# The end of a graph-attention loop written out as one list of stages

## Chip, cores, metric

The kernel runs on one core of a Trainium2 chip. The metric is device time in microseconds of one execution; the median of three runs is 2806.0 us (2797.12 to 2806.96).

## What is computed

One graph layer over 12500 nodes of 128 features and 200000 edges that are sorted by their destination:

```
h = relu(layernorm(x))
Q = h @ W_Q.T;  K = h @ W_K.T
score[e] = (Q[dst[e]] . K[src[e]]) / sqrt(128) * exp(-edge_weight[e])
keep the 16 highest scores of each destination node
alpha = softmax of the kept scores over a node's edges
agg[n] = sum over its kept edges of alpha[e] * (h[src[e]] @ W_msg.T)
out = x + relu(h @ W_self.T + agg)
```

## The kernel before

A preparation computes h into a table in DRAM (`h_tab`) and lays the edge arrays out by columns. Then the edges are worked off in G = 112 groups. A group is 14 chunks of 128 edges, and since a node's edges may reach into the next group, 15 chunks are looked at (`chunks[g]`); the last group, called L = G - 1 = 111 here, has 9. In what follows L-1, L-2 and so on are the groups ahead of it.

A group goes through these stages, each a small function that emits the instructions of one or two engines (lines of the profile in brackets):

- `gather` [L399, POOL]: one indirect DMA for each chunk, 128 rows of `h_tab` by the chunk's source indices; `let_go` [L414, DVE] copies the indices that release them. Group g's are issued during the loop pass of group g-2.
- `load_nodes`, `load_dst` [SP's DMAs], `far_of`, `to_edges` [L466, L471, ACT] and `places` [L477, L479, DVE]: the one-hot matrices that take node values to edges and edges to slots.
- `q_to_edges(g, b)` [L490, PE]: the query rows for four chunks, three matmuls a chunk, into one of three PSUM banks q. `scores(g, b)` [L500, DVE]: one instruction a chunk, the product of gathered row, query row and decay, summed. The instruction waits for its chunk's gathered rows.
- `scores_in_slots` [L508, DVE], `slots_by_node` [L513, L515, PE], `slots_out` [L520, ACT], `node_by_slots` [L523, PE]: the scores of a node's edges side by side in one row, in PSUM tile e.
- `best` [L529 to L541, DVE]: the 16 highest, and a mask with the negated maximum (`km`). `sum_of_exps` [L546, ACT], `one_over_sum` [L551, L552, DVE].
- `kept_to_edges` [L558, PE]: mask and maximum back to the edges, in PSUM tile x, of which there is one. `on_edges` [L564 to L571, DVE] reads it, `exps` [L575, ACT], `weights` [L579, L580, DVE] writes the weights into `alz`, of which there are two.
- `sums(g, 0)`, `sums(g, 1)` [L590, PE]: the weighted sums of gathered rows, two matmul passes a chunk, the first half of the chunks and the second. `sums_out` [L595, ACT], `sums_turned` [L598, PE], `sums_turned_out` [L602, ACT], `products` [L605, L606, PE], `output` [L610, DVE].
- `store` [L616 and L619]: a direct DMA on SP's queue for all but the last four groups; for groups L-3 to L a scattered DMA on POOL's queue, whose rows the program can't tell apart from those of other stores, so that each waits for the store ahead of it to land.

The order of instructions on each engine is the order in which the stages are called (`tc.manual_schedule()`, L386). It is written out by hand in the loop at L630: pass i calls stages of groups i+3 (loads) down to i-5 (output), interleaved so that each engine has work of several groups. The function `at` leaves out a stage whose group doesn't exist. The loop runs from -3 to G+5; passes L to L+6 have no gather left to release and wind the open groups up, each pass calling the stages in the same order: for group L the pass i = L, for L-1 `slots_by_node` first in that pass, for L-2 `best` to `on_edges`, for L-3 `weights` and `sums`, for L-4 `sums_turned` and `products`, for L-5 `output` and `store`. Where pass L has two stages of one engine, one group's waits hold up the other's[...].

After the loop comes a branch at L685 that is not taken with these inputs.

Of the kernel before, what the change touches and what calls it, by code (L numbers as in the profile page):

```python
# [38 lines left out]
TAIL = 4  # L39
# [35 lines left out]
def gnn_layer(  # L75
# [32 lines left out]
    LAST = N - (NT - 1) * P  # L108
    CH = -(-M // P)
    G = -(-CH // GC)  # L110
    assert G > TAIL
    EG = GC * P

    CPR = 13
# [271 lines left out]
    with tc.tile_pool(name="win", bufs=2) as win, tc.manual_schedule():  # L386
# [96 lines left out]
        def q_to_edges(g, b):  # L483
            j0, j1 = 4 * b, min(4 * b + 4, chunks[g])
            if j0 >= j1:
                return
            T[g]["pq", b] = pq = bank("q", 3)
            for j in range(j0, j1):
                for k in range(3):
                    nc.tensor.matmul(pq[:, (j - j0) * P:(j - j0 + 1) * P],  # L490
                                     lhsT=T[g]["to_e"][:, j * P:(j + 1) * P], rhs=upper(T[g]["q"][:, k, :]),
                                     start=(k == 0), stop=(k == 2))
# [18 lines left out]
        def slots_by_node(g):  # L511
            n = chunks[g]
            nc.tensor.matmul(et[0:KM + 1, 0:WW], lhsT=zrow[:, 0:KM + 1], rhs=zrow, start=True, stop=False)  # L513
            for j in range(n):
                nc.tensor.matmul(et[0:KM + 1, STEP * j:STEP * j + WN], lhsT=sl1[g % 2][:, j, :],  # L515
                                 rhs=T[g]["ow"][:, j, :], start=False, stop=(j == n - 1))

        def slots_out(g):
            T[g]["eT"] = win.tile([KM + 1, P], F32, name="eT")
            nc.scalar.copy(T[g]["eT"], et[0:KM + 1, PRE:PRE + P])  # L520

        def node_by_slots(g):
            nc.tensor.transpose(et[:, 256:256 + KM + 1], T[g]["eT"], ident[0:KM + 1, 0:KM + 1])  # L523


        def best(g):
            pt = et[:, 256:256 + KM + 1]
            ell = win.tile([P, KM], F32, name="ell")
            nc.vector.tensor_scalar(ell, slots, pt[:, KM:KM + 1], NEG, op0=OP.is_ge, op1=OP.mult)  # L529
            nc.vector.tensor_add(ell, ell, pt[:, 0:KM])  # L530
            T[g]["v16"] = v16 = win.tile([P, TOPK], F32, name="v16")
            rest = win.tile([P, KM], F32, name="rest")
            nc.vector.max(v16[:, 0:8], ell)
            nc.vector.match_replace(rest, v16[:, 0:8], ell, NEG)
            nc.vector.max(v16[:, 8:16], rest)
            nc.vector.match_replace(rest, v16[:, 8:16], rest, NEG)
            T[g]["km"] = km = win.tile([P, KM + 3], F32, name="km")
            nc.vector.tensor_scalar(km[:, KM:KM + 1], v16[:, 0:1], FLOOR, -1.0, op0=OP.max, op1=OP.mult)  # L538
            nc.vector.tensor_tensor(km[:, 0:KM], rest, ell, op=OP.not_equal)
            for k in range(KM, KM + 2):  # L540
                nc.vector.tensor_sub(km[:, k + 1:k + 2], km[:, k:k + 1], upper(km[:, k:k + 1]))  # L541
# [7 lines left out]
        def one_over_sum(g):  # L549
            T[g]["rden"] = rden = win.tile([P, 1], F32, name="rden", bufs=4)  # L550
            nc.vector.tensor_scalar(rden, T[g]["den"], 0.25, None, op0=OP.max)  # L551
            nc.vector.reciprocal(rden, rden)  # L552
# [8 lines left out]
        def on_edges(g):  # L561
            n, px = chunks[g], T[g]["px"]
            T[g]["up"] = up = win.tile([P, NJ], F32, name="up", bufs=3)
            nc.vector.tensor_reduce(up[:, 0:n], px[:, 0:n, KM:KM + 3], axis=AX.X, op=OP.add)  # L564
            nc.vector.tensor_add(up[:, 0:n], up[:, 0:n], T[g]["s"][:, 0:n])

            nc.vector.tensor_scalar(up[:, 0:n], up[:, 0:n], 0.0, None, op0=OP.min)  # L567
            mine = win.tile([P, NJ, KM], F32, name="mine", bufs=1)
            nc.vector.tensor_tensor(mine[:, 0:n, :], px[:, 0:n, 0:KM], T[g]["po"][:, 0:n, :], op=OP.mult)
            T[g]["kept"] = kept = win.tile([P, NJ], F32, name="kept", bufs=3)  # L570
            nc.vector.tensor_reduce(kept[:, 0:n], mine[:, 0:n, :], axis=AX.X, op=OP.add)  # L571

        def exps(g):
            n = chunks[g]
            nc.scalar.activation(T[g]["up"][:, 0:n], T[g]["up"][:, 0:n], AF.Exp)  # L575

        def weights(g):
            n, kept = chunks[g], T[g]["kept"]
            nc.vector.tensor_tensor(kept[:, 0:n], T[g]["up"][:, 0:n], kept[:, 0:n], op=OP.mult)  # L579
            nc.vector.tensor_tensor(alz[g % 2].rearrange("e (j w) -> e j w", w=WW + STEP)[:, 0:n, 0:WN],  # L580
                                    T[g]["ow"][:, 0:n, :], bc(kept[:, 0:n], WN), op=OP.mult)


        def sums(g, part):
            n = chunks[g]
            if part == 0:
                T[g]["pa"] = bank("a", 1)
            half = n // 2
            for j in range(half) if part == 0 else range(half, n):
                nc.tensor.matmul(T[g]["pa"][:, 0:P], lhsT=alz[g % 2][:, WW * j + PRE:WW * j + PRE + P],  # L590
                                 rhs=rows_of(g, j), start=(j == 0), stop=(j == n - 1))

        def sums_out(g):
            T[g]["agn"] = win.tile([P, D], F32, name="agn")
            nc.scalar.activation(T[g]["agn"], T[g]["pa"][:, 0:P], AF.Copy, scale=T[g]["rden"])  # L595

        def sums_turned(g):
            nc.tensor.transpose(so[:, 2 * P:3 * P], T[g]["agn"], ident)  # L598

        def sums_turned_out(g):  # L600
            T[g]["aggT"] = win.tile([P, P], F32, name="aggT")
            nc.scalar.copy(T[g]["aggT"], so[:, 2 * P:3 * P])  # L602

        def products(g):
            nc.tensor.matmul(so[:, 3 * P:4 * P], lhsT=T[g]["hT"], rhs=wselfT, start=True, stop=False)  # L605
            nc.tensor.matmul(so[:, 3 * P:4 * P], lhsT=T[g]["aggT"], rhs=wmsgT, start=False, stop=True)  # L606

        def output(g):
            T[g]["o"] = win.tile([P, D], F32, name="o")
            nc.vector.scalar_tensor_tensor(T[g]["o"], so[:, 3 * P:4 * P], 0.0, T[g]["x_t"],  # L610
                                           op0=OP.max, op1=OP.add)

        def store(g):

            if g < G - TAIL:
                nc.sync.dma_start(out[ds(start_of(g, 0, N - P), P), :], T[g]["o"])  # L616
            else:
                k = g - (G - TAIL)
                nc.gpsimd.indirect_dma_start(  # L619
                    out=out[:, :], out_offset=bass.IndirectOffsetOnAxis(ap=idxo[:, k:k + 1], axis=0),  # L620
                    in_=T[g]["o"], in_offset=None, bounds_check=N - 1, oob_is_err=False)

        def at(g, stage, *args):
            if 0 <= g < G:
                stage(g, *args)
# [1 line left out]
        for g in range(min(2, G)):  # L627
            gather(g, 0, own[g], lambda j: idx_all[:, GC * g + j:GC * g + j + 1])

        for i in range(-3, G + 6):  # L630
            at(i + 3, load_nodes)
            at(i + 2, load_dst)

            more = (lambda k: let_go(i + 2, k)) if 0 <= i < G - 2 else (lambda k: None)
            at(i, q_to_edges, 0)
            at(i - 5, output)
            at(i - 5, store)
            at(i - 3, weights)
            more(0)
            at(i - 4, sums_turned)  # L640
            at(i - 4, sums_turned_out)
            at(i + 1, q_out)
            at(i, q_to_edges, 1)
            at(i + 1, far_of)
            at(i - 1, slots_by_node)
            at(i + 1, places)
            more(1)
            at(i - 2, best)
            more(2)
            at(i - 2, sum_of_exps)  # L650
            at(i - 1, slots_out)
            at(i, q_to_edges, 2)
            at(i + 2, h_turned)
            at(i, scores, 0)
            more(3)
            at(i + 1, to_edges)
            at(i + 1, q_parts)
            at(i + 2, h_turned_out)
            at(i - 3, sums, 0)
            at(i - 2, kept_to_edges)  # L660
            at(i, scores, 1)
            more(4)
            at(i, q_to_edges, 3)
            at(i - 2, one_over_sum)
            at(i - 3, sums, 1)
            at(i, scores, 2)
            at(i - 2, on_edges)
            more(5)
            at(i - 4, products)
            at(i - 3, sums_out)  # L670
            at(i - 2, exps)
            at(i, scores, 3)
            at(i, scores_in_slots)
            more(6)
            at(i - 1, node_by_slots)
            at(i + 2, q_made)


    GR = 4
# [178 lines left out]
```

## Time and profile before

| | |
|---|---|
| median of three runs | 2806.0 us |
| lowest, highest | 2797.12, 2806.96 us |
| profiled execution, its own time | 2125.5 us |
| its span, first to last instruction | 2123.7 us |
| mean granted clock of TensorE | 0.795 |
| busy: POOL, DVE, PE, ACT | 1544.1, 1488.2, 1312.0, 626.7 us |
| last gather issued (L399) | 2084.51 us |
| last score (L500) | 2087.57 us |
| last output row block (L610) | 2109.77 us |
| last store issued (L619) | 2111.38 us |

The profiled execution was 680.5 us shorter than the median of the runs; the page does not say where the difference lies. All places in time below are of the profiled execution, counted from its first instruction. A row of a group gives line, engine, operation, the tiles written and read, how often, the busy time, the mean of one, and the idle time of the engine ahead of them with what ended it. A row in order of time begins with start and duration in us and may end with the engine's idle time ahead of it, in brackets, and the instruction that ended it.

### The profile page before, as it was taken

How to read it: one execution, taken by the hardware profiler on the slowest of the kernel's cores; microseconds unless marked ns; L12 is line 12 of the kernel's file. 1: busy time of each engine (PE TensorE's matmuls, PEld its weight loads, DVE VectorE, ACT ScalarE, POOL GpSimd, SP SyncE). 2: the span in 40 equal slices, each digit the busy share in tenths (PEclk: the TensorE clock that was granted, in tenths of full speed). 3: DMA queues.
4: the chain of work that ended last, by engine and by line, in shares of the span. 5: the costliest groups of instructions: out<-in, count | busy, mean ns of one | idle time of the engine just before them, and what ended most of it. 6: DMA issues, size and time to landing. Idle time of an engine off the chain costs nothing. (4 is left out here: it accounts for less than half of the span.)

```text
span 2123.7 us, 43559 instructions
## 1 busy us (share of the span) xinstructions
PE 1312.0 (62%) x14574; PEld 1210.1 (57%) x14575; DVE 1488.2 (70%) x7474; ACT 626.7 (30%) x1225; POOL 1544.1 (73%) x1585
## 2 busy tenths in 40 slices
PE   1166666666666666666666666666666666666665
PEld 1155566555555655555555656565666666565654
DVE  7667677777776777767777767677777776777764
ACT  3442222222222222222222222222222222222220
POOL 1477777777777777777777777777777777777773
PEclk9977877877777877877777777777777787877787
DMA  8453343333343343333333334334433343333420
GB/s 220 146 162 116 119 120 119 120 119 119 120 119 119 116 122 115 115 112 119 118 119 119 119 119 120 119 119 120 120 119 120 119 120 120 119 119 119 120 67 24
DMA packets 118805, 253.18 MB, mean 119 GB/s; under 512 B 33030, under 2 KB 76297, under 8 KB 118558
## 3 DMA queue, kind: packets, MB, share of 16 engines
q1 hardware_dynamic: 67336, 144.92, 19.7%
q0 software_dynamic: 50144, 102.74, 19.1%
q10 hardware_dynamic: 1094, 2.69, 0.5%
q8 instruction: 115, 1.88, 0.4%
q14 instruction: 116, 0.95, 0.1%
HBM read 236.40 MB, written 14.40 MB: 118 GB/s over the span
## 5 line engine op out<-in xcount | busy, mean ns | idle before, releaser
L399 POOL DMA_INDIRECT hs<-h_tab,ix x1535 | 1495.9, 975 | 467.8 <-issue 335.9
L500 DVE SCALAR_TENSOR_TENSOR prod<-hs,dec_all,q 128x128 f32<-128x128 f32 x1674 | 516.9, 345 | 334.3 <-DMA hs<-h_tab,ix 319.1
L490 PE MATMUL q<-q,to_e 128*128 128x128 bf16 x5022 | 464.2, 254 | 33.1 <-DVE prod L500 32.3
L598 PE MATMUL s<-ident,agn 128*128 128x128 f32 x112 | 49.3, 440 | 662.2 <-DVE kept L579 661.7
L490 PEld LDWEIGHTS <-to_e 128*128 128x128 bf16 x5022 | 410.1, 116 | 56.0 <-issue 39.8
L590 PE MATMUL a<-hs,alz 128*128 128x128 f32 x3348 | 425.8, 281 | 0.8 <-DVE alz L580 0.8
L598 PEld LDWEIGHTS s<-ident,agn 128*128 128x128 f32 x112 | 20.2, 180 | 678.4 <-issue 676.7
L590 PEld LDWEIGHTS a<-hs,alz 128*128 128x128 f32 x3348 | 404.4, 197 | 1.2 <-DVE alz L580 1.1
L515 PE MATMUL e<-ow,sl 128*41 128x40 f32 x3348 | 251.3, 265 | 8.4 <-DVE sl L508 8.4
L515 PEld LDWEIGHTS e<-ow,sl 128*41 128x41 f32 x3348 | 235.7, 184 | 23.6 <-DVE sl L508 9.2
L466 ACT ACTIVATE far<-dstb,nb 128x1920 bf16<-128x1920 int32 x112 | 212.9, 1901 | 5.1 <-DMA dstb<-in_dst_dram 5.1
L471 ACT ACTIVATE to_e<-far 128x1920 bf16<-128x1920 bf16 x112 | 201.2, 1796 | 0.1
L602 ACT COPY aggT<-s 128x128 f32<-128x128 f32 x112 | 29.8, 266 | 507.8 <-PE s L598 507.8
L529 DVE TENSOR_SCALAR ell<-slots,e 128x40 f32<-128x40 f32 x112 | 28.3, 253 | 205.3 <-PE e L515 192.6
L546 ACT ACTIVATE e<-v,km 128x16 f32<-128x16 f32 x112 | 34.4, 308 | 363.5 <-DVE km L538 363.5
L500 DVE DVE_READ_ACCUMULATOR prod<-hs,dec_all,q 128x1 f32 x1674 | 139.1, 83 | 0.2
L414 DVE COPY ix<-idx_all 128x2 int32<-128x2 int32 (+1 forms) x768 | 132.7, 173 | 0.0
L575 ACT ACTIVATE up<-up 128x15 f32<-128x15 f32 x112 | 24.1, 215 | 336.5 <-DVE up L567 336.4
L595 ACT ACTIVATE agn<-a,rden 128x128 f32<-128x128 f32 x112 | 41.2, 368 | 209.8 <-PE a L590 209.8
L508 DVE TENSOR_TENSOR sl<-po,s 128x600 f32<-128x600 f32 x112 | 87.5, 781 | 3.9
L580 DVE TENSOR_TENSOR alz<-ow,kept 128x600 f32<-128x600 f32 x112 | 87.5, 781 | 3.8
L399 POOL DMA_INDIRECT hs<-h_tab,idx_all x28 | 33.7, 1203 | 77.6 <-DMA x_end<-zpad 69.4
(150 smaller groups left out, 1562.7 us busy)
## 6 DMA issues: line engine op xcount, KB each, us to landing
dstb<-in_dst_dram SPq DMA_DIRECT2D x111, 960.0 KB
hs<-h_tab,ix POOLq DMA_INDIRECT x1535
h_r<-h_tab SPq DMA_DIRECT2D x112, 64.0 KB
x_t<-in_x_dram SPq DMA_DIRECT2D x108, 64.0 KB
out_dram<-o SPq DMA_DIRECT2D x108, 64.0 KB
xg<-in_x_dram SPq DMA_DIRECT2D x10, 560.0 KB
h_tab<-xg SPq DMA_DIRECT2D x10, 560.0 KB
dst_r<-in_dst_dram ACTq DMA_DIRECT2D x1, 803.2 KB
```

What stands on the lines that cost most here:

```text
L399: nc.gpsimd.indirect_dma_start(out=T[g]["hs"][:, j, :], out_offset=None, in_=h_tab[0:N, :], in_offset=bass.IndirectOffsetOnAxis(ap=index(j ...
L414: nc.vector.tensor_copy(ix[:, j0:j1], idx_all[:, GC * g + j0:GC * g + j1])
L466: nc.scalar.activation(T[g]["far"][:, 0:n], T[g]["dstb"][:, 0:n], AF.Square, bias=nb[:, g:g + 1])
L471: nc.scalar.activation(T[g]["to_e"][:, 0:n], T[g]["far"][:, 0:n], AF.Relu, bias=1.0, scale=-1.0)
L490: nc.tensor.matmul(pq[:, (j - j0) * P:(j - j0 + 1) * P], lhsT=T[g]["to_e"][:, j * P:(j + 1) * P], rhs=upper(T[g]["q"][:, k, :]), start=(k ...
L500: nc.vector.scalar_tensor_tensor(prod, rows_of(g, j), dec_all[:, c:c + 1], T[g]["pq", b][:, (j % 4) * P:(j % 4 + 1) * P], op0=OP.mult, op1 ...
L508: nc.vector.tensor_tensor(sl1[g % 2][:, 0:n, 0:KM], T[g]["po"][:, 0:n, :], bc(T[g]["s"][:, 0:n], KM), op=OP.mult)
L515: nc.tensor.matmul(et[0:KM + 1, STEP * j:STEP * j + WN], lhsT=sl1[g % 2][:, j, :], rhs=T[g]["ow"][:, j, :], start=False, stop=(j == n - 1))
L580: nc.vector.tensor_tensor(alz[g % 2].rearrange("e (j w) -> e j w", w=WW + STEP)[:, 0:n, 0:WN], T[g]["ow"][:, 0:n, :], bc(kept[:, 0:n], WN) ...
L590: nc.tensor.matmul(T[g]["pa"][:, 0:P], lhsT=alz[g % 2][:, WW * j + PRE:WW * j + PRE + P], rhs=rows_of(g, j), start=(j == 0), stop=(j == n ...
L595: nc.scalar.activation(T[g]["agn"], T[g]["pa"][:, 0:P], AF.Copy, scale=T[g]["rden"])
L598: nc.tensor.transpose(so[:, 2 * P:3 * P], T[g]["agn"], ident)
```

## The change

The loop stops after pass G - 2, so the passes G - 1 to G + 5 are gone. In their place stands one list of calls for group L and all stages that are then open of the groups L-5 to L-1. Some small functions bundle stages: `turned` is `sums_turned` and `sums_turned_out`; `all_sums` both halves of `sums` and `sums_out`; `to_rows` is `products`, `output` and `store`; `to_nodes` the three stages that bring scores into node rows; `kept_on_edges` is `one_over_sum`, `on_edges` and `exps`. The stages themselves, their instructions, tiles and buffers are as before.

```diff
-    assert G > TAIL
+    assert G > TAIL + 2
...
-        for i in range(-3, G + 6):
+        for i in range(-3, G - 1):
...
+        L = G - 1
+        blocks = -(-chunks[L] // 4)
...
+        q_to_edges(L, 0)
+        output(L - 5)
+        store(L - 5)
+        weights(L - 3)
+        turned(L - 4)
+        slots_by_node(L - 1)
+        slots_out(L - 1)
+        best(L - 2)
+        sum_of_exps(L - 2)
+        q_to_edges(L, 1)
+        node_by_slots(L - 1)
+        to_rows(L - 4)
+        all_sums(L - 3)
+        kept_to_edges(L - 2)
+        best(L - 1)
+        sum_of_exps(L - 1)
+        scores(L, 0)
+        kept_on_edges(L - 2)
+        turned(L - 3)
+        kept_to_edges(L - 1)
+        scores(L, 1)
+        weights(L - 2)
+        all_sums(L - 2)
+        to_rows(L - 3)
+        for b in range(2, blocks):
+            q_to_edges(L, b)
+            scores(L, b)
+        scores_in_slots(L)
+        to_nodes(L)
+        kept_on_edges(L - 1)
+        turned(L - 2)
+        best(L)
+        sum_of_exps(L)
+        weights(L - 1)
+        kept_to_edges(L)
+        all_sums(L - 1)
+        to_rows(L - 2)
+        kept_on_edges(L)
+        turned(L - 1)
+        weights(L)
+        all_sums(L)
+        to_rows(L - 1)
+        turned(L)
+        to_rows(L)
```

More of the change, by code (lines that the diff above doesn't have):

```diff
@@ L676, in gnn_layer, with turned, all_sums, to_rows @@
             at(i + 2, q_made)
+        L = G - 1
+        blocks = -(-chunks[L] // 4)
+        def turned(g):
+            sums_turned(g)
+            sums_turned_out(g)
+        def all_sums(g):
+            sums(g, 0)
+            sums(g, 1)
+            sums_out(g)
+        def to_rows(g):
+            products(g)
+            output(g)
+            store(g)
+        def to_nodes(g):
+            slots_by_node(g)
+            slots_out(g)
+            node_by_slots(g)
+        def kept_on_edges(g):
+            one_over_sum(g)
+            on_edges(g)
+            exps(g)
+        q_to_edges(L, 0)
[42 more added lines that the diff above has]
+        to_rows(L)
     GR = 4
```

## Prediction

> **What bounds the kernel now.** I read the page first, then the waits before the gathers, then the order of time over the last 50 us, because the edit touches nothing earlier.
>
> ```profile
> span 2123.7 us, 43559 instructions
> ...
> POOL 1477777777777777777777777777777777777773
> ...
> L399 POOL DMA_INDIRECT hs<-h_tab,ix x1535 | 1495.9, 975 | 467.8 <-issue 335.9
> ```
>
> The row gathers bound the loop: 1535 of them at 975 ns, with 467.8/1535 = 0.30 us before each, make 1.25 us apiece. DVE (70%) and PE (62%) have slack in every iteration, POOL has none. The edit leaves every gather where it was, and the last one is issued at 2084.51 us. So only what lies after about 2078 us can move: 2123.7 - 2078.2 = 45.5 us, 2% of the span. There the order of time shows what ends last:
>
> ```profile
> 2082.88 0.25 DVE L529 TENSOR_SCALAR ell<-slots,e 128x40 f32<-128x40 f32 x1 [3.50 <-PE e L515]
> ...
> 2084.51 0.97 POOL L399 DMA_INDIRECT hs<-h_tab,ix  x1 [0.30 <-DVE km L538]
> ...
> 2087.57 0.35 DVE L500 SCALAR_TENSOR_TENSOR prod<-hs,dec_all,q 128x128 f32<-128x128 f32 x1 [0.23 <-PE a L590]
> ...
> 2098.10 0.29 DVE L610 SCALAR_TENSOR_TENSOR o<-s,x_t 128x128 f32<-128x128 f32 x1 [0.21 <-PE s L606]
> ...
> 2099.35 1.83 PE L590 MATMUL a<-hs,alz 128*128 128x128 f32 x14 [0.51 <-DVE alz L580]
> ...
> 2101.55 2.03 PE L590 MATMUL a<-hs,alz 128*128 128x128 f32 x16
> ...
> 2105.05 2.27 PE L590 MATMUL a<-hs,alz 128*128 128x128 f32 x18 [0.26 <-DVE alz L580]
> ...
> 2107.87 0.29 DVE L610 SCALAR_TENSOR_TENSOR o<-s,x_t 128x128 f32<-128x128 f32 x1 [2.87 <-ACT agn L595]
> 2108.44 0.98 POOL L619 DMA_INDIRECT out_dram<-o,idxo  x1 [2.56 <-DVE o L610]
> ...
> 2111.38 0.98 POOL L619 DMA_INDIRECT out_dram<-o,idxo  x1 [1.96 <-issue]
> ```
>
> What to see: the last score (L = 111, chunk 8) runs at 2087.57, about 3.1 us after its gather was issued; the last sums end at 2107.3, 19.7 us later; then come product, output and two scattered stores. The two last stores stand 2108.44 to 2111.38 = 2.94 us apart although the last row block was ready at 2110.06: each waits until the one before it has landed. After 2111.38 there are 12.3 us that no step of the edit touches. So the question is one thing: how long after its gather does the last score run, and how long from there to the last sums.
>
> **The change, worked through.** Nothing is added or removed in kind; the built program has the same stages, in another order on PE, DVE and ACT. POOL and SP keep theirs: the last gathers, then four scattered stores. I walk the new list by hand from 2078.19, where both orders are still the same (L508 of L-1 ends its slot), engine by engine in program order. A stage starts when its engine is free and its input is there plus 0.1 us handing over. Durations, slot to slot, from this trace: on DVE `best` 2.0 (2082.88 to 2084.85), one score 0.27, the reciprocal 0.27, `on_edges` 2.0, with its reads of PSUM tile x over after 1.3 (2087.84 to 2089.14), `weights` 0.9, `output` 0.2. On PE `sums` of 15 chunks 3.7 at full clock, `slots_by_node` 2.5 at half clock for 15 chunks and 1.15 for 9, a block of 12 score products 1.4 at half clock, `kept_to_edges` 0.5, `products` 0.6 or 1.05 at half clock. Walked the same way, the old order puts its last store at 2111.75, where the trace has 2111.38; the method is 0.4 us long.
>
> 1. Slots ahead of the score products (a gain). `slots_by_node(L-1)` no longer queues behind the 1.4 us of q_to_edges(L,1). `best(L-2)`, which waited 3.50 us for it, starts at 2081.6 instead of 2082.9.
> 2. Early close of L-4 (a gain). node_by_slots(L-1) and products(L-4) follow at once, so output(L-4) runs at 2084.5 (before 2090.31) and best(L-1) at 2084.7 to 2086.7 (before 2092.24). The store of L-4, on SP's queue, goes out 5.8 us earlier; nothing else is queued there, and the POOL store of L-3, which must follow its landing, comes 13 us later.
> 3. The whole of `sums(L-3)` in front of kept_to_edges(L-2) (a loss). Before, the latter stood between the two halves, at 2085.56. Now PE does 2084.4 to 2088.35 first. So on_edges(L-2) starts at 2088.9 (before 2087.84), with DVE idle for 0.9.
> 4. A new wait on PE: kept_to_edges(L-1) writes the one buffer of x that on_edges(L-2) is still reading; it stands from 2089.2 to 2090.3. Queued behind it are sums(L-2), products(L-3) and q_to_edges(L,2); none could start before weights(L-2) anyway, so this costs nothing.
> 5. scores(L,1) at 2090.95, weights(L-2) 2092.0 to 2093.0 (before 2090.5 to 2091.5), sums(L-2) 2093.1 to 2096.8, products(L-3) to 2097.35, output(L-3) at 2097.4 (before 2098.10).
> 6. The heart of it: the list puts output(L-3) on DVE, and sums(L-2) and products(L-3) on PE, **ahead** of the last score. DVE waits from 2093.0 to 2097.4 for PE. So the last score runs at 2097.6, 10.1 us later than in the trace, although its row has long landed.
> 7. What is saved behind it: before, 19.7 us passed from that score's start to the last sums' end. Now: slots multiplied 2098.0 to 2098.45; slots_by_node, its copy and the transpose end at 2100.4 beside on_edges(L-1), 2098.7 to 2100.7; best(L) to 2102.7; weights(L-1) to 2103.7; sums(L-1) 2103.75 to 2107.5; products(L-2), output(L-2) at 2108.1; only behind that, in DVE's queue, on_edges(L), 2108.6 to 2110.1, and weights(L) to 2110.9; sums(L) 2111.0 to 2113.2. That is 15.6 us, 4.1 less.
> 8. The end is the old one: output(L-1) at 2113.9, its store at 2114.5, the last store 2.94 us later: 2117.4.
>
> Sum: +10.1 at the last score, -4.1 behind it, so +6.0 us at the last store (2117.4 against 2111.38), all at full clock after 2085.
>
> **The clock[...].** [...] The new list has no idle stretch of PE above 2.8 us (2090.8 to 2093.1, 2100.7 to 2103.75 with a short stage in it)[...]
>
> ```profile
> 2088.00:2090.00 2.00, 0.60 (x5) 0.36 (x3) 1.90 (x6) 0.58 (x2) 0.00 (x0) 1.00 0.00 0
> 2090.00:2092.00 2.00, 1.26 (x20) 1.09 (x20) 1.46 (x4) 0.27 (x1) 0.00 (x0) 0.93 0.14 41
> 2092.00:2094.00 2.00, 2.00 (x12) 1.93 (x10) 1.59 (x11) 0.06 (x1) 0.00 (x0) 0.50 0.01 4
> 2094.00:2096.00 2.00, 2.00 (x25) 1.99 (x25) 0.76 (x6) 0.49 (x3) 0.00 (x0) 0.72 0.01 4
> ```
>
> These are stretches of 2 us; after the engines' busy times comes the granted clock. PE was idle for 2.15 us only, and 3.2 us at half clock followed, under a sums block. The new list has gaps like that in two or three places. One such stretch in the walk puts the last store at 2118.3 to 2118.9, two or three at 2120. I take one, the number that the old tail had: 2118.3, less the method's 0.4: **+6.5 us**.
>
> **Bounds of what the trace does not show.** Whether a q-bank or `o` buffer is waited for in the new order: the nearest row is the 0.23 us before the last score; 0 to +0.5, not below 0, since no buffer comes free sooner than its reader; I take 0. Instruction supply with another order: the instruction counts are within three rows; 0.
>
> **From the profile to the median.** The profiled execution took 2125.5 us, span 2123.7 and 1.8 around it; the median of the runs shown is 2806.0, 680.5 more. The page doesn't say where those are. I carry the difference over in microseconds: 2806.0 + 6.5 = 2812.5. If they are spread over the loop as slower gathers (680.5/1563 = 0.44 us each, 1.69 a gather), the last row lands about 3.5 us later against the work queued ahead of it, step 6 costs that much less, and the change comes to +1 to +3. If it is a slower PE, steps 3, 5 and 7 stretch: +8.
>
> **Rivals.**
> - The last score isn't on the path. If the last row lands ten or more us later relative to the queues, step 6 is covered, and what is left is the shorter chain behind the score: 19.8 us from last score to last store (2097.6 to 2117.4) against 23.8 (2087.57 to 2111.38), 4 us faster: 2802. For it: the unexplained 680 us. Against: the profile has that row landed by 2087.6, and 1.69 us a gather gives 3.5 of the 10 needed.
> - The cold tail, the slower side beyond what can be told apart. If the chopped matmul stretches keep the clock at half from 2085 to the end, each 15-chunk sums costs 3.0 more (14 matmul halves in 3.14 against 1.73, times 30/14), three of them 9.0, the last 1.8: 6.0 + 10.8 = 16.8, 2823. [...] Against it: from 2095 the old tail ran at 1.00 with gaps of 0.3 to 0.7 us.
> - It does nothing, the two effects cancelling as in the slower-gather case: 2807.
>
> **How the numbers follow.** A measurement of this kernel tells some 0.5%, 14 us, from no change; the whole chain after the last gather is 27 us, so a gain of 14 would need half of it gone. Chances: the walk, +3 to +10, 0.60; cancelling, 0 to +3, 0.20; faster by up to 6, 0.10; cold tail 0.07; something that no row shows 0.03. Faster by over 0.5% 0.02, within 0.90, slower 0.08. The range reaches from the faster case, less 3 us for the spread of the runs, to the cold tail: 2799 to 2823.
>
> **What would show it.** In the changed profile: L529 of L-2 at about 2081.6; output L610 of L-4 near 2084.5; the last score after 2096 with L610 just ahead of it on DVE and a wait of 4 us there for PE L606; sums(L) ending near 2113; the last L619 near 2118; gathers and 95% of the slices as before. The prediction is wrong if the last score runs before 2092, if the stores end before 2111, or if a slice before 2078 changes.

## The result and the profile after

The changed kernel takes 2819.1 us (median of 20 runs) against 2806.3 (20 runs): ratio 1.0041, 95% interval 1.0029 to 1.0054, so 8 to 15 us more. It is slower, by a little less than the 0.5% that the prediction could tell from no change, and by about twice the 6.5 us forecast.

One thing is needed to read the profiles: the same program takes some 2122 us on some chips (a short execution, in what follows) and some 2800 us on others (a long one). The first profile of before came from a 2125.5 us execution, the one of after from a 2821.4 us execution. So only the end is compared between them, on a clock of its own: **the tail**, from the start of L508 of group L-1 (2077.49 in before, 2764.02 in after), where both orders are still the same, to the start of the last L619. One difference stays: in before the last gather is issued 7.0 us after the tail begins (2084.51), in after 17.4 us ahead of it (2746.61).

Order of time at the end of the changed kernel, the lines that answer to those shown of before:

```profile
2767.25 0.25 DVE L529 TENSOR_SCALAR ell<-slots,e 128x40 f32<-128x40 f32 x1 [1.34 <-ACT eT L520]
...
2777.93 6.44 PE L590 MATMUL a<-hs,alz 128*128 128x128 f32 x30 [2.24 <-DVE alz L580]
...
2784.93 0.29 DVE L610 SCALAR_TENSOR_TENSOR o<-s,x_t 128x128 f32<-128x128 f32 x1 [7.05 <-ACT agn L595]
2785.13 0.34 DVE L500 SCALAR_TENSOR_TENSOR prod<-hs,dec_all,q 128x128 f32<-128x128 f32 x1
2785.50 1.01 POOL L619 DMA_INDIRECT out_dram<-o,idxo  x1 [37.94 <-DVE prod L500]
...
2790.35 0.40 PE L558 MATMUL x<-km,to_e 128*128 128x43 bf16 x9 [2.48 <-DVE km L541]
2791.25 4.98 PE L590 MATMUL a<-hs,alz 128*128 128x128 f32 x30 [0.51 <-DVE alz L580]
2796.78 0.29 DVE L610 SCALAR_TENSOR_TENSOR o<-s,x_t 128x128 f32<-128x128 f32 x1 [5.58 <-ACT agn L595]
2799.72 3.10 PE L590 MATMUL a<-hs,alz 128*128 128x128 f32 x18 [2.20 <-DVE alz L580]
2803.77 0.29 DVE L610 SCALAR_TENSOR_TENSOR o<-s,x_t 128x128 f32<-128x128 f32 x1 [4.11 <-PE s L606]
...
2807.29 0.98 POOL L619 DMA_INDIRECT out_dram<-o,idxo  x1 [1.97 <-issue]
```

The tail is 2807.29 - 2764.02 = 43.3 us, against 33.9 before. Two things to see. The three `sums` take 6.44, 4.98 and 3.10 us; the prediction had 3.7, 3.7 and 2.2. And DVE stands ahead of each L610 while PE makes the sums (7.05, 5.58, 4.11 us), while PE stands idle ahead of each sums, waiting for DVE: 2.24 us ahead of sums(L-2), 2.48 ahead of kept_to_edges(L) (L558), which comes just before sums(L-1), and 2.20 ahead of sums(L). They take turns. Over the whole tail, what DVE waited for:

```profile
DVE o L610 <- ACT agn L595: 12.6, 2, 7.0
DVE o L610 <- PE s L606: 4.6, 2, 4.1
DVE o L610 <- ACTq L758: 1.7, 1, 1.7
```

That is 18.9 us at L610. In a second profile of before it is 5.7:

```profile
DVE o L610 <- ACT agn L595: 2.9, 1, 2.9
DVE o L610 <- ACTq L685: 1.6, 1, 1.6
DVE o L610 <- PE s L606: 1.2, 2, 0.7
```

The clock in the tail of after, in stretches of 2 us. After the length of each come the busy times of PE, PEld, DVE, ACT and POOL (instructions in brackets), then the granted clock, the DMA share and GB/s:

```profile
2774.00:2776.00 2.00, 0.71 (x16) 0.44 (x15) 1.91 (x5) 0.43 (x3) 0.00 (x0) 1.00 0.00 0
2776.00:2778.00 2.00, 0.07 (x1) 0.07 (x1) 1.84 (x10) 0.00 (x0) 0.00 (x0) 0.77 0.04 8
2778.00:2780.00 2.00, 2.00 (x9) 2.00 (x10) 0.00 (x0) 0.00 (x0) 0.00 (x0) 0.50 0.00 0
2780.00:2782.00 2.00, 2.00 (x12) 2.00 (x11) 0.00 (x0) 0.00 (x0) 0.00 (x0) 0.50 0.00 0
2782.00:2784.00 2.00, 2.00 (x12) 2.00 (x12) 0.00 (x0) 0.00 (x0) 0.00 (x0) 0.53 0.00 0
2784.00:2786.00 2.00, 1.17 (x12) 0.90 (x10) 1.04 (x5) 0.37 (x1) 0.50 (x1) 1.00 0.00 0
```

PE waits 2.24 us for the weights, the clock falls to 0.50, and nearly the whole of sums(L-2) (2777.93 to 2784.37) runs at it.

### The profile page after: what moved, and what is told of

It reads as the page before. It is cut to its first block, busy times and chain, and to the rows that moved or that the text cites. A ratio compares the mean times of both kernels' runs of the same rounds, so it can differ in the third digit from the quotient of the medians.

```text
span 2819.7 us, 43556 instructions
## 1 busy us (share of the span) xinstructions
PE 1646.5 (58%) x14574; PEld 1418.4 (50%) x14575; DVE 1480.7 (53%) x7474; ACT 616.1 (22%) x1225; POOL 1553.2 (55%) x1585
## 3 DMA queue, kind: packets, MB, share of 16 engines
q0 software_dynamic: 50144, 102.74, 13.8%
## 5 line engine op out<-in xcount | busy, mean ns | idle before, releaser
L490 PE MATMUL q<-q,to_e 128*128 128x128 bf16 x5022 | 564.6, 260 | 397.8 <-issue 374.2
L590 PE MATMUL a<-hs,alz 128*128 128x128 f32 x3348 | 623.5, 351 | 124.1 <-issue 114.0
L490 PEld LDWEIGHTS <-to_e 128*128 128x128 bf16 x5022 | 427.5, 117 | 478.5 <-issue 463.4
L590 PEld LDWEIGHTS a<-hs,alz 128*128 128x128 f32 x3348 | 580.1, 261 | 163.9 <-issue 151.0
L500 DVE SCALAR_TENSOR_TENSOR prod<-hs,dec_all,q 128x128 f32<-128x128 f32 x1674 | 490.6, 344 | 210.6 <-remote 135.9
L529 DVE TENSOR_SCALAR ell<-slots,e 128x40 f32<-128x40 f32 x112 | 29.3, 262 | 531.6 <-remote 306.9
L515 PEld LDWEIGHTS e<-ow,sl 128*41 128x41 f32 x3348 | 217.9, 161 | 143.1 <-issue 126.7
L610 DVE SCALAR_TENSOR_TENSOR o<-s,x_t 128x128 f32<-128x128 f32 x112 | 32.4, 290 | 295.8 <-issue 274.1
L558 PE MATMUL x<-km,to_e 128*128 128x43 bf16 x1674 | 70.3, 192 | 61.0 <-DVE km L541 48.8
L558 PEld LDWEIGHTS <-to_e 128*128 128x128 bf16 x1674 | 65.3, 104 | 70.9 <-DVE km L541 51.3
L564 DVE TENSOR_REDUCE up<-x 128x15 f32<-128x45 f32 x112 | 22.6, 202 | 148.9 <-remote 83.8
L508 DVE TENSOR_TENSOR sl<-po,s 128x600 f32<-128x600 f32 x112 | 87.6, 782 | 12.9 <-DVE prod L500 9.9
```

The costliest lines, as they stand in the source:

```text
L490: nc.tensor.matmul(pq[:, (j - j0) * P:(j - j0 + 1) * P], lhsT=T[g]["to_e"][:, j * P:(j + 1) * P], rhs=upper(T[g]["q"][:, k, :]), start=(k ...
L500: nc.vector.scalar_tensor_tensor(prod, rows_of(g, j), dec_all[:, c:c + 1], T[g]["pq", b][:, (j % 4) * P:(j % 4 + 1) * P], op0=OP.mult, op1 ...
L508: nc.vector.tensor_tensor(sl1[g % 2][:, 0:n, 0:KM], T[g]["po"][:, 0:n, :], bc(T[g]["s"][:, 0:n], KM), op=OP.mult)
L558: nc.tensor.matmul(px[:, j, 0:KM + 3], lhsT=T[g]["to_e"][:, j * P:(j + 1) * P], rhs=upper(T[g]["km"]), start=True, stop=True)
```

## The experiments

The theories: **A**, the prediction's step 6, the last score queued behind output(L-3) is the cost. **B**, the list puts each group's `on_edges`, `weights`, whole `sums` and rows in series, so that PE and DVE take turns; the last score only rides along. **C**, the gaps that B opens on PE set its clock to half (0.50 in the stretches above) under the sums. The times in this table are us of the tail or from its start, and the granted clock decides over some us of each (sums(L-2): 3.62 us at 1.00 in filled, 6.44 us nearly all at 0.50 in after); DVE's waiting is that at L610. The second column says whether the profile is of a short or a long execution. Before and after as they stand were never profiled in the same kind; the nearest to the changed kernel in a short execution is filled_first, 44.1.

| kernel | execution | tail | last score at | sums of L-2, L-1, L | DVE waiting |
|---|---|---|---|---|---|
| before, three profiles | short | 33.9, 33.7, 33.8 | 9.9 to 10.1 | in halves | 5.7 (second) |
| after, two profiles | long | 43.3, 45.3 | 21.1, 22.4 | 6.44, 4.98, 3.10 (first) | 18.9 (first) |
| score_early | short | 41.3 | 13.9 | 5.24, 5.13, 2.96 | |
| edges_first | short | 40.9 | 20.0 | 5.24, 6.37, 2.27 | |
| filled | short | 38.2 | 18.6 | 3.62, 3.62, 2.27 | 12.9 |
| filled_first | short | 44.1 | 19.5 | 3.62, 6.33, 4.21 | |
| filled_edges | long | 37.0 | 18.3 | 3.62, 3.62, 2.22 | 12.3 |
| filled_both | long | 36.2 | 13.8 | 3.62, 3.62, 2.22 | 12.0 |
| filled_ahead | short | 36.7 | 15.2 | 3.62, 3.59, 2.22 | 8.5 |
| before_filled | short | 32.7 | 9.9 | in halves | |
| relisted | long | 26.0 | 8.8 | in halves | 4.5 |

**before_again, before_look.** The kernel before, unchanged, profiled twice more.

> The kernel before, unchanged, for a second profile. The first one was of an execution of 2125.5 us, the median of the runs is 2806; the changed kernel's profile is of one of 2821.4, with PE idle for 'issue' ahead of its matmuls. If the 680 us are in the loop and not in the end, a profile of a 2806 us execution shows the gathers at more than 1.25 us apiece, PE waiting for issue, and the tail (from the start of L508 of L-1 to the last store) still at 34 us, as in the short execution; up to 37 if the half clock falls on more of the sums. If part of the 680 us is in the tail, the tail is longer than that, and the change's 43.3 us has to be compared with it.

> The kernel before once more, for a profile of an execution of some 2800 us, if the chip of this call is one where it takes that long (the two looks so far were of 2125). The tail from L508 of L-1 to the last store was 33.9 and 33.7 us there. If the slow issue of PE instructions stays in the loop, the tail is 33 to 36 here too and the 9 to 13 us between the kernels are the two tails; if it lengthens the tail of before, it is above 36.

Both fell on chips where it takes 2122 to 2130 us, so a tail of before in a long execution was never seen, and whether it is 33.8 there too stays open.

**after_again.** The changed kernel, timed in 18 runs beside 39 of before.

> The changed kernel, unchanged, on the chip of this call and timed beside before. On a chip where before takes some 2122 us (gathers at 1.25 us, the last one issued 7 us after L508 of L-1), the prediction's walk has a tail of 40 us (all sums warm) and the profile of the 2821 us execution has 43.3. If the tail alone makes the difference, it is 42 to 44 here too, with two of the sums at half clock, and the time is 8 to 11 us over before. If the 2821 us execution's slow issue of PE instructions had a part in its 43.3, the tail is 40 or less here and the time 5 to 6 us over before.

The executions were long ones again (before 2787.2): ratio 1.0032, interval 1.0021 to 1.0042, 6 to 12 us. The tail, 45.3, is above the expected 42 to 44. Of the 2.0 us between the two profiles of this kernel, 1.2 are there by output(L-4) (5.7 and 6.9 us into the tail) and 0.8 lie in the wait ahead of the last store (1.97 and 2.77 us); so tails that differ by 2 us or less need not differ by the order. In neither of the two tails does PE wait for issue, so the slow issue described at the end of this document does not lengthen them directly. They are 9.5 and 11.5 us over before's 33.8, the times 8 to 15 and 6 to 12 us: the tail is enough to account for the whole of the difference, if before's is 33.8 in a long execution too.

**score_early.** Step 6 undone.

```diff
         weights(L - 2)
+        for b in range(2, blocks):
+            q_to_edges(L, b)
+            scores(L, b)
+        scores_in_slots(L)
         all_sums(L - 2)
         to_rows(L - 3)
-        for b in range(2, blocks):
-            q_to_edges(L, b)
-            scores(L, b)
-        scores_in_slots(L)
```

> The changed kernel with only the last scores (q_to_edges(L,2), scores(L,2), scores_in_slots(L)) moved ahead of sums(L-2) and the rows of L-3. Tail of the changed kernel: 43.3 us. Theory A (the prediction's step 6: the last score queued behind output(L-3) is what costs): the score runs some 6 us earlier and the tail falls by about 6, to 37, time near that of before. Theory B (what costs is that each group's on_edges, weights, whole sums and rows now follow one another, the score only rides along): the score runs earlier, but the tail falls by 1 or less. Theory C (the half clock under the sums): no change beyond where the clock happens to fall, 2 us either way.

The last score, and the last store:

```profile
2089.56 0.34 DVE L500 SCALAR_TENSOR_TENSOR prod<-hs,dec_all,q 128x128 f32<-128x128 f32 x1
...
2116.98 0.98 POOL L619 DMA_INDIRECT out_dram<-o,idxo  x1 [1.96 <-DVE o L610]
```

With the tail's start at 2075.68, the last score runs 7 us earlier and the tail falls by 2 (41.3), of which 1.2 us are shorter sums (13.3 for the three against 14.5); the time stays at 1.0038 of before (1.0026 to 1.0051). A expected 6 and fails: the score's place is worth a small part of its delay. B's "1 or less" is not met as it stands; a gain of 2 us lies within what two profiles of one kernel differ by, and filled_both below, with the clock up, is the cleaner test.

**edges_first.** DVE makes the last group's weights before it waits for the rows of L-2.

```diff
-        to_rows(L - 2)
         kept_on_edges(L)
+        to_rows(L - 2)
```

> The changed kernel with one swap: kept_on_edges(L) ahead of the rows of L-2, so that DVE does not wait for sums(L-1) before it makes the last group's weights. Tail of the changed kernel: 43.3 us. Theory B: weights(L) is ready while sums(L-1) still runs, PE goes from one sums to the next without the 2.2 us of waiting, tail 41 to 41.5. Theory A: no change, the score stays where it is. Theory C: 2 us either way.

Sums of L-1 and L in the profile of edges_first:

```profile
2102.49 6.37 PE L590 MATMUL a<-hs,alz 128*128 128x128 f32 x30 [0.39 <-DVE rden L551]
...
2110.34 2.27 PE L590 MATMUL a<-hs,alz 128*128 128x128 f32 x18 [0.26 <-DVE alz L580]
```

The 2.2 us ahead of sums(L) are gone, as B expected, and with them the half clock under it (2.27 against 3.10). But sums(L-1) fell into it instead, 6.37 against 4.98. With the clock moving, 2.4 us can't be put down to the order alone. Hence the next.

**filled.** The gaps of PE stuffed with matmuls whose result nobody reads, so that the clock stays up and the order is seen alone.

```diff
+        def fill(n):
+            pq = bank("q", 3)
+            for _ in range(n):
+                nc.tensor.matmul(pq[:, 0:P], lhsT=T[L]["to_e"][:, 0:P], rhs=upper(T[L]["q"][:, 0, :]),
+                                 start=True, stop=True)
...
         kept_to_edges(L - 1)
+        fill(30)
...
         turned(L - 2)
+        fill(50)
...
         turned(L - 1)
+        fill(30)
         weights(L)
```

> The changed kernel with idle stretches of PE filled by 30, 50 and 30 matmuls that nobody reads (into score banks that are free, after kept_to_edges(L-1), turned(L-2) and turned(L-1)); no other order is changed and the work it adds lies where PE waited 2.2, 3.3 and 2.2 us. Tail of the changed kernel: 43.3 us, with the sums of L-2, L-1 and L at 6.4, 5.0 and 3.1 us instead of 3.7, 3.7 and 2.2. Theory C (gaps of that length tip the clock to half, and that is what the walk missed): the sums fall to 3.7 to 4, and the tail by 3 to 5, to 38.5 to 40. Theories A and B alone: the sums stay as long as they are or the tail falls by less than 1.

The sums of filled, all at full clock:

```profile
2087.99 3.62 PE L590 MATMUL a<-hs,alz 128*128 128x128 f32 x30 [0.53 <-DVE alz L580]
...
2098.48 3.62 PE L590 MATMUL a<-hs,alz 128*128 128x128 f32 x30 [0.32 <-DVE alz L580]
...
2105.57 2.27 PE L590 MATMUL a<-hs,alz 128*128 128x128 f32 x18 [0.49 <-DVE alz L580]
```

The three sums are 14.5 - 9.5 = 5.0 us shorter than in after, the tail 5.1: C holds for that part. More work on PE made the tail shorter. After's profile is of a long execution and this one of a short one; filled_first, short too and with only one gap filled, has 14.2 us of sums and a tail of 44.1 against the 9.5 and 38.2 here. The times don't show the gain: the ratio to before is 1.0029 (1.0020 to 1.0038), still slower, and its interval overlaps those of the changed kernel.

**before_filled.** The same filling in the old order, at its one gap of some 2.2 us (2.15, 2.76 and 2.07 in the three profiles of before).

```diff
         for i in range(-3, G + 6):
+            if i == G:
+                fill(30)
```

> The kernel before with 30 matmuls that nobody reads at the head of the pass after L, where PE waited 2.2 us for DVE and 3 us at half clock followed under the first half of sums(L-2) (14 passes in 3.25 and 2.89 us instead of 1.8). If a gap of 2.2 us is what sets the clock back, these 14 passes take 1.8 us and the tail is 32.3 to 32.8 instead of 33.8. If it is not ([...]the clock falls by itself), the half clock stays or moves and the tail is 33.5 to 34.5.

```profile
2088.27 1.83 PE L590 MATMUL a<-hs,alz 128*128 128x128 f32 x14
```

The first half of sums(L-2) takes 1.83 us at a granted clock of 1.00, against 3.25, 2.89 and 3.27 in three profiles of before, and the tail is 32.7. So the old order paid 1.1 us to the clock where the new one pays 5.1, and with the clock up in both, both short, the new order is 38.2 - 32.7 = 5.5 us longer.

**filled_first.** Only the first of the three fillings.

> The changed kernel with only the first of the three fillings (30 matmuls after kept_to_edges(L-1), where PE waits 2.2 us for weights(L-2)). If each gap sets the clock back for the sums that follow it, sums(L-2) take 3.6 us instead of 5.2 to 6.4, sums(L-1) stay at 5 or fall by half of that, and the tail is 40 to 42 instead of 43.3 to 45.3. If the three gaps only work together, or the filling works in another way, sums(L-2) stay at 5 or more.

Sums of L-2, L-1 and L:

```profile
2089.66 3.62 PE L590 MATMUL a<-hs,alz 128*128 128x128 f32 x30 [0.53 <-DVE alz L580]
...
2100.15 6.33 PE L590 MATMUL a<-hs,alz 128*128 128x128 f32 x30 [0.39 <-DVE alz L580]
...
2109.97 4.21 PE L590 MATMUL a<-hs,alz 128*128 128x128 f32 x18 [2.21 <-DVE alz L580]
```

A miss: sums(L-2) came out at full clock (3.62 us) as expected, but the half clock (0.50 from 2100.58 to 2104.58 and again from 2110.58) moved on to the next two, 14.2 us for the three together as against 14.5, and the tail didn't fall. Closing one gap of three bought nothing here.

**filled_edges, filled_both, filled_ahead.** With the clock up, the swaps one on top of the other: that of edges_first; then also that of score_early; then also `kept_on_edges(L-1)` and `weights(L-1)` ahead of the sums of L-2.

```diff
         scores_in_slots(L)
+        kept_on_edges(L - 1)
+        weights(L - 1)
         all_sums(L - 2)
         to_rows(L - 3)
         to_nodes(L)
-        kept_on_edges(L - 1)
         turned(L - 2)
...
-        weights(L - 1)
```

> The filled kernel with the swap of edges_first: kept_on_edges(L) ahead of the rows of L-2. With the clock full in both, the order is seen alone: the filled one has a tail of 38.2 us. Theory B: sums(L) no longer waits for weights(L), tail 36 to 36.8. Theory A (the last score's place is the cost): 38.

> The filled kernel with both swaps, kept_on_edges(L) ahead of the rows of L-2, and the last scores ahead of sums(L-2) and the rows of L-3. Theory A: the second swap gives back most of the 4.4 us that the filled kernel's tail (38.2) is over that of before (33.8), so some 34. Theory B: 0.8 us less than with the first swap alone, 35.5 to 36.

> filled_both (tail 36.2 us) with kept_on_edges(L-1) and weights(L-1) also ahead of sums(L-2) and the rows of L-3, so that DVE makes the next weights before it stands behind output(L-3). Theory B (PE and DVE take turns, because a group's output stands at the head of DVE's queue while PE makes its sums): sums(L-1) start 1 to 1.5 us earlier, tail 34.5 to 35.2, and DVE's waiting at L610 falls by as much from 12.0 us. If the rest of the 2.4 us to before has another cause, the tail stays at 36.

The tails of filled, filled_edges, filled_both and filled_ahead are 38.2, 37.0, 36.2 and 36.7. Of the first swap's 1.2 us, 0.4 are there at the start of sums(L-2) (14.25 and 13.89 us into the tail), ahead of where the two lists first differ; that leaves 0.8, less than B expected. The second, between two profiles on one chip, gains 0.8 as B expected, where A expected a tail of 34: with the clock up the last score's place is worth no more than this. The third missed what B expected: DVE's waiting at L610 fell from 12.0 to 8.5 us, but waits at L529 (3.8 in all against 1.4) and L564 (1.5 against 0.4) took its place, so that less waiting at L610 is not by itself a shorter tail. The tail also began with a longer half clock (0.50 to 0.55 over its first 8 us, where filled_both has 0.50 to 0.68 over 4), output(L-4) at 6.9 instead of 5.8; from there to the end it is 29.8 against 30.4. No single swap carries B; 3.5 us to the filled old order are left and are not split up further.

**relisted.** The whole list written anew from the walk: PE gets the small stages of other groups between the halves of each sums, DVE gets the next weights before it stands at an output, and the rows of L-1 go out between the halves of sums(L). Its second half:

```
        sums(L - 1, 0)
        best(L)
        products(L - 2)
        output(L - 2)
        kept_to_edges(L)
        on_edges(L)
        one_over_sum(L - 1)
        exps(L)
        sums(L - 1, 1)
        sums_out(L - 1)
        sums_turned(L - 1)
        sum_of_exps(L)
        store(L - 3)
        sums_turned_out(L - 1)
        store(L - 2)
        weights(L)
        sums(L, 0)
        products(L - 1)
        output(L - 1)
        store(L - 1)
        sums(L, 1)
        one_over_sum(L)
        sums_out(L)
        sums_turned(L)
        sums_turned_out(L)
        products(L)
        output(L)
        store(L)
```

> The same stages in another list: kept_to_edges, on_edges and weights of L-2 early, the sums of each group in halves with the next group's small PE stages between them, the last score right after its row can have landed, each group's rows as soon as its sums allow, the rows of L-1 between the halves of sums(L). If what costs is that a group's chain of on_edges, weights, sums and rows stands in series (theory B), interleaving it more than before did gives a tail below that of before: walked by hand, 27 us with the clock full, 29 with it half in places, against 33.8; 5 to 7 us (0.2 to 0.3%) faster than before. If the tail is bound by the last score's landing and the chain behind it (theory A), it is not below 32.

Tail 26.0, ratio to before 0.9979 (0.9971 to 0.9987), so 4 to 8 us faster, on the chip where the changed kernel was 6 to 12 us slower. What DVE waited for in its tail:

```profile
DVE o L610 <- ACTq L764: 2.5, 1, 2.5
DVE o L610 <- PE s L606: 2.0, 2, 1.8
```

The same stages, the same engines: 4.5 us of waiting at L610 instead of 18.9, and all sums at full clock (1.80 to 2.03 us a half of 14 or 16 passes). B and C fit both signs. But this list moved everything at once, the last score too (8.8 us into the tail), and it is a long execution, in which the last row was gathered before the tail began; so it shows what another order is worth, not which of its moves is worth how much. The ratio, from runs on one chip, carries that; the tail of 26.0 is set against 33.8 from short executions.

## Why the prediction was right, and where its sum failed

- **Only the end can move: nothing speaks against it.** The tails differ by 9.5 and 11.5 us, the times by 8 to 15 and 6 to 12. The sign named for it, the slices before 2078, can't be read from after's profile, which is of a long execution. On one chip, with short ones, L508 of L-1 starts at 2077.99 in before_again and at 2075.68, 2076.35 and 2073.74 in score_early, edges_first and filled: no later with the new list.
- **From the short execution to the long ones: right in its result, open in its cases.** POOL bounds the loop in the execution profiled, not in those timed: in after's profile POOL is busy 55% of the time, in before's 73%. The difference carried over in microseconds held, since 686.5 of the 696.0 us between the two spans are there when the tail begins. The case "slower gathers, the last row lands later" (+1 to +3), and with it the rival "the last score isn't on the path", did not come about: the last row was asked for 17.4 us before the tail, not later, so that rival was not tested. The case "slower PE" (+8) had the loop right, where PE waits for issue (374.2 us ahead of L490 in after), but not the tail, where it doesn't: what stretched the steps there was the clock, 0.80 over the tail of after against 0.93 over that of filled.
- **Steps 1 and 2 (early slots, early rows of L-4): right.** L529 of L-2 at +3.2 in the tail (predicted +4.1, before +5.4), output(L-4) at +5.7 (predicted +7.0, before +12.8).
- **Steps 3 to 5: right in kind, except the loss of step 3.** on_edges(L-2) came at +9.8 in the first profile and +11.0 in the second (predicted +11.4, before +10.4), so its sign is not settled. The wait for x in step 4 was 0.98 us (predicted 1.1). sums(L-2) start at +13.9 (predicted +15.6), but output(L-3) comes at +20.9 (predicted +19.9), for the half clock under those sums.
- **Step 6, "the heart of it": right as a place, wrong as a cause.** The last score runs at +21.1 (predicted +20.1), behind L610, as the prediction put it. But moving it 7 us forward gave 2 us, and 0.8 with the clock up. The prediction summed a delay and a saving along one chain (+10.1 - 4.1) and took the delay for the cause. Its walk was better than this label: with the clock up, 15.5 us pass in filled from the last score to the end of the last sums (step 7: 15.6). What the profiles show in its place is PE and DVE taking turns over three groups, which step 7 describes and books as a saving; one part of it, output(L-2) ahead of on_edges(L), is worth 0.8 us, and how the rest splits is open.
- **Step 8: right.** The last two stores stand 2807.29 - 2804.34 = 2.95 us apart (predicted 2.94), in the second profile 3.75.
- **The clock: mis-sized.** The order term, +6.0, or 5.6 less the method's 0.4, sets a new tail all at full clock against the old one as it was, with its half-clock stretch. Measured like that it is 38.2 - 33.8 = 4.4, and 5.5 with the clock up in both. For the clock in the new order the prediction added 0.9 (2118.3 against 2117.4): "I take one, the number that the old tail had". It measured 5.1, 4.0 more than the 1.1 in the old order: there are three gaps (2.24, 2.48 and 2.20 us), and three half-clock stretches, each under a sums. The order came out 1.2 us smaller than forecast and the clock 4.2 larger, so by luck the one error made good a part of the other. That brings the whole to +9.5 in the tail, at the top of the walk's +3 to +10, while the times, 8 to 15, reach beyond it; both stay inside the range 2799 to 2823. The prediction had the row that shows 0.50 after a gap of 2.15 us, named two or three places like it, and counted one. Its cold-tail rival, at +16.8, was the same half clock carried too far.
- **The gaps and the clock.** With the clock up the tail is the 38.2 us of filled; as the list stands it was 43.3. Gaps of 2.24, 2.48 and 2.20 us with a few short stages around them were each followed by half clock, and filling them kept the clock at 1.00 from the first filled gap to the last sums. In relisted a gap of 2.26 us ahead of L513 was not followed by it: the clock is 1.00 in every stretch of its tail. So what length of gap brings the half clock was not shown.

## What to carry to other kernels

When a pipeline is drained, "each stage as soon as its group allows" is not the same as keeping two engines busy: ask of each instruction at the head of a queue what it waits for and what stands behind it, over all open groups, and try the other engine's next input ahead of the output that waits for this one's last. One such swap gained 0.8 us here and another nothing that could be measured; only the list rewritten as a whole was faster. Price a wait that is opened on PE twice, once as itself and once as the half clock that may follow (here 5.1 us after three gaps of 2.2 to 2.5 us), and count every such gap. A late step is a cause only if moving it alone moves the end.

## What the runs showed of the hardware

- Gaps of 2.15, 2.76 and 2.07 us on PE were followed by about 3 us at a granted clock of 0.50 in the three profiles of before; with 30 small matmuls in the gap (before_filled) the clock stayed at 1.00 and the 14 passes behind it took 1.83 us instead of 2.89 to 3.27. After a gap of 2.26 us in relisted it was 1.00 too. The price is not fixed: after gaps of 2.24 and 2.23 us the same sums(L-2) took 6.44 us in after and 5.24 in edges_first, against 3.62 at full clock. In the new order, closing one of three gaps only moved the half clock to the next sums (14.2 against 14.5 us for the three).
- In the long executions PE stands still between matmuls. Score products in the middle of the changed kernel:

```profile
2076.61 0.28 PE L490 MATMUL q<-q,to_e 128*128 128x128 bf16 x2 [1.15 <-issue]
2078.05 0.37 PE L490 MATMUL q<-q,to_e 128*128 128x128 bf16 x2 [1.17 <-issue]
```

Two matmuls, then 1.2 us in which PE waits for nothing that the profile shows; the idle time that this kind of wait leaves ahead of L490's matmuls comes to 374.2 us over that execution, while in the 2125 us execution of before all idle time ahead of them is 33.1 us. The gathers wait 502.1 us for DVE's scores there (34.1 in the short one). So the 680 us or so between the two kinds of execution lie ahead of the tail; why one chip does this and another doesn't was not tried and stays open.
